# Transposing normalised rows with 32 by 32 squares on VectorE and DMAs through DRAM, instead of on TensorE

## The chip, the cores and the metric

The kernel runs on one core of a Trainium2 chip. The metric is the device time of one execution in microseconds (us), the median of several runs. A profiled execution gives the trace from which the rows below are taken.

## The reference

A "macaron" block on x of shape (B, L, D) = (4, 1024, 256): half a feed-forward network, a convolution over positions, half a feed-forward network, each behind a layer norm without weights.

```python
def ffn(x):                                     # weights are -1, 0 or 1, times a scale per output
    h = silu(tlin(x, w1_w, w1_s)) * tlin(x, w2_w, w2_s)      # 256 -> 1024, twice
    h = gelu(tlin(h, h1_w, h1_s))                            # 1024 -> 1024
    h = gelu(tlin(h, h2_w, h2_s))                            # 1024 -> 1024
    return tlin(h, w3_w, w3_s)                               # 1024 -> 256

def mixer(x):                                   # S4D: K is made from log_dt, A, C
    y = irfft(rfft(x^T, 2L) * rfft(K, 2L))[:, :, :L]         # along the positions
    return gelu(y^T) @ W.T + b

x = x + 0.5 * ffn(layernorm(x))
x = x + mixer(layernorm(x))
x = x + 0.5 * ffn(layernorm(x))
```

## The kernel before

**Blocks.** The 4096 positions are cut in eight blocks of 512 tokens. The first network goes over them in turn "f" (f0 to f7, from `x` to a DRAM tile `x1`), the second in turn "g" (g0 to g7, from the DRAM tile `x2` to the output). The blocks run in one loop, f0 to g7; `ffn` does one of them. A row of x (one token, 256 features) has to be normalised along its features, with tokens on the partitions, and then multiplied with weights that want features on the partitions. So each block's normalised rows are transposed.

**Positions.** A block lies in SBUF as 128 partitions of four rows (`JT` = 4). `positions` says which tokens these are: partition p holds tokens 8p to 8p+3 (first half of a sequence, even blocks) or 8p+4 to 8p+7 (second half). The mixer `mix(b)` uses the same places: its result rows j, j+1 of every partition are stored to `x2` in four stores (j = 0, 2, 4, 6), so an even block of turn g reads what the first two of them wrote.

**Parts.** An fp32 activation is split in two parts that TensorE multiplies one after the other: part 0 is a cast (`fp32r`), part 1 is what the cast lost, which `low_part` computes on VectorE (L240). The tiles `xt` (two of 128x512), `ha` and `h` (eight each) have both parts. So a matmul group of a layer of 1024 inputs has 16 matmuls of 128x512.

**A block.** `ffn` issues for m = 0..7 the products pa and pb of the first layer; then layers 2 and 3, eight groups each (`p_f`, `p_g`, L267, called by `linear`); after each group ScalarE does the gelu (L299) and the cast (L301), VectorE the low part. G0 to G7 below stand for the ends of layer 3's eight groups on TensorE. Then come 64 matmuls of 128x256 for the result (`po`, L323), which take h as their stationary operand, and `finish`: scaling on VectorE, the residual's addition on POOL, a store by SP.

**What is put between.** After every group `tick()` advances one step of `aside`, the generator that makes the spectrum of the convolution's kernel (`kernel_spectrum`, beside f2 to f4) and then runs `mix(0)` to `mix(3)`; sometimes also a step of `weight_checks`, which loads weights again (`given`) and compares them. `spectrum` loads four matrices of 256 KB (`m_m2_0` is matrix 0 of mix 2; `m_k_0` and so on, of the kernel's spectrum, come in two halves of 128 KB) on SP's queue, in the order 0, 2, 1, 3, and multiplies rows with them (`pf_m`, `pf_k`, L621: 8 matmuls, one product). The mixer's rows `xm` go through the same `norm`. During layer 3, `ahead()` advances `prepare` for the next block: `load_x` (one DMA of 512 KB), `norm` in two steps, and at the call after the last group `transposed`:

```python
pts = [bank(f"pt_{name}_{k}") for k in range(DC)]       # two PSUM banks
for k, i in order:                                       # 2 x 4 squares of 128 x 128
    nc.tensor.transpose(
        pts[k][:, i * P : (i + 1) * P], xn[:, i, k * P : (k + 1) * P], ident   # L248
    )
...
nc.vector.tensor_copy(xt[k][:, 0, :], pts[k])            # L258
last = low_part(xt[k], pts[k])                           # L240
```

The first block has no predecessor; its transposes come ahead of the loop. The execution takes the branch with split parts; a second branch without them is for other weights.

**Order.** A scheduler fixes the order on every engine when the kernel is built, from the program's order and its own estimate of when each piece will be ready. At run time each engine, and each queue of DMAs that SP issues, goes strictly through its list. A tile pool has a limited number of buffers for a tag (`xb` three, `half` 19, PSUM eight banks).

Of the kernel before, what the change touches and what calls it, by code (L numbers as in the profile page):

```python
# [11 lines left out]
F32 = mybir.dt.float32  # L12
# [5 lines left out]
P = 128  # L18
B, L, D = 4, 1024, 256
HID = 1024  # L20
J = L // P
DC = D // P
KH = HID // P
TB = 512
JT = TB // P
N2 = 32
DD = D // 2

# [65 lines left out]
def macaron_layers(  # L94
# [23 lines left out]
    nc = tc.nc  # L118
    split = bad is not None
    wide = F32R if split else F32  # L120
    parts = 2 if split else 1
    keep = ctx.enter_context(tc.tile_pool(name="keep", bufs=1))
    work = ctx.enter_context(tc.tile_pool(name="work", bufs=2))
    small = ctx.enter_context(tc.tile_pool(name="small", bufs=2))
    dram = ctx.enter_context(tc.tile_pool(name="dram", bufs=1, space=bass.MemoryType.DRAM))
# [6 lines left out]
    def half(name, *shape, dtype=F32):  # L132

        return work.tile([P, *(shape or (512,))], dtype, tag="half", name=name, bufs=19)

    def ring(name, *shape, dtype=F32):

        return work.tile([P, *shape], dtype, tag="ring", name=name, bufs=15)
# [5 lines left out]
    ident = keep.tile([P, P], F32, name="ident")  # L144
# [12 lines left out]
    x1 = dram.tile([B, L, D], F32, name="x1")  # L157
    x2 = dram.tile([B, L, D], F32, name="x2")

    k_hat = dram.tile([2 + len(PAIRS), 2, P, 2, D], F32, name="k_hat")  # L160

    def column(i):
# [2 lines left out]
    def positions(t, b, j, n=2):  # L165
        return t[b].rearrange("(p j) d -> p j d", j=J)[:, j : j + n, :]

    def load_x(t, blk, name, queue=nc.sync):
        b, g = divmod(blk, J // JT)
        xb = work.tile([P, JT, D], F32, tag="xb", name=name, bufs=3)  # L170
        queue.dma_start(xb, positions(t, b, g * JT, JT))
        return xb

    def rows(w):
# [4 lines left out]

    x_first = work.tile([P, JT, D], F32, tag="xb", name="x_f0", bufs=3)  # L180
    for i, queue in ((0, nc.sync), (2, nc.scalar)):
        queue.dma_start(x_first[:, i : i + 2, :], positions(x, 0, i))
    eps = small.tile([P, 1], F32, name="eps", bufs=1)
    nc.vector.memset(eps, EPS)

# [52 lines left out]
    def low_part(t, src):  # L238

        return tt(t[:, 1, :], src, t[:, 0, :].bitcast(F32), ALU.subtract)  # L240

    def transposed(xn, name, first=False):


        pts = [bank(f"pt_{name}_{k}") for k in range(DC)]
        order = [(k, i) for k in range(DC) for i in range(JT)]
        for k, i in sorted(order, key=lambda o: o[1]) if first else order:
            nc.tensor.transpose(  # L248
                pts[k][:, i * P : (i + 1) * P], xn[:, i, k * P : (k + 1) * P], ident
            )  # L250
        xt = [ring(f"xt_{name}_{k}", parts, TB, dtype=wide) for k in range(DC)]
        last = None
        if first:
            last = nc.vector.tensor_copy(xt[0][:, 0, :], pts[0])  # L254
            nc.scalar.copy(xt[1][:, 0, :], pts[1])
        for k in range(DC):
            if not first:
                nc.vector.tensor_copy(xt[k][:, 0, :], pts[k])  # L258
            if split:
                last = low_part(xt[k], pts[k])  # L260
        return (xt, last) if first else xt

    def linear(ps, w, m, acts):
        n = len(acts)
# [10 lines left out]
    def ffn(xt, src, dst, blk, name, tick, ahead, final):  # L275

        ha = []
        for m in range(KH):  # L280
            pa, pb = bank(f"pa_{name}_{m}"), bank(f"pb_{name}_{m}")
            linear(pa, w1_sb, m, xt)
            linear(pb, w2_sb, m, xt)
            g = half(f"g_{name}_{m}")
            t = ring(f"ha_{name}_{m}", parts, TB, dtype=wide)
            nc.scalar.activation(g, pa, AF.Silu, scale=sc_sb[:, 0, m : m + 1])  # L286
            stt(g if split else t[:, 0, :], pb, sc_sb[:, 1, m : m + 1], g, ALU.mult, ALU.mult)
            if split:
                nc.scalar.copy(t[:, 0, :], g)
                low_part(t, g)  # L290
            ha.append(t)
        for layer, w in ((2, h1_sb), (3, h2_sb)):
            hb = []
            for m in range(KH):
                ps = bank(f"p{layer}_{name}_{m}")
                linear(ps, w, m, ha)
                t = ring(f"h{layer}_{name}_{m}", parts, TB, dtype=wide)
                g = half(f"g{layer}_{name}_{m}") if split else t[:, 0, :]
                nc.scalar.activation(g, ps, AF.Gelu, scale=sc_sb[:, layer, m : m + 1])  # L299
                if split:  # L300
                    nc.scalar.copy(t[:, 0, :], g)  # L301
                    low_part(t, g)
                hb.append(t)
                if layer == 3:
                    ahead()
                if m < KH - 1:
                    tick()
            ha = hb
        ahead(last=True)
        tick()  # L310
        b, g = divmod(blk, J // JT)
        rest = []
        for i in range(0, JT, 2):
            xr = half(f"xr_{name}_{i}", 2, D)
            nc.sync.dma_start(xr, positions(src, b, g * JT + i))
            rest.append(xr)

        def result(ps, i, n):

            for e in range(n):  # L320
                for k in range(KH):
                    for part in range(parts):
                        nc.tensor.matmul(  # L323
                            ps[:, e * D : (e + 1) * D],
                            ha[k][:, part, (i + e) * P : (i + e + 1) * P],
                            w3_sb[:, k, :],
                            start=(k == 0 and part == 0),
                            stop=(k == KH - 1 and part == parts - 1),
                        )

        def finish(ps, y, xr, i, n, add_on):
            stt(
                y,
                ps.rearrange("p (e d) -> p e d", e=n),
                0.5,
                w3s_sb[:, None, :].to_broadcast([P, n, D]),
                ALU.mult,
                ALU.mult,
            )
            add_on.tensor_tensor(y, xr, y, ALU.add)  # L340
            nc.sync.dma_start(positions(dst, b, g * JT + i, n), y)

        for i in range(0, JT, 2):
            y = half(f"y_{name}_{i}", 2, D)
            if final and i + 2 == JT:
                for e in range(2):
                    ps = bank(f"po_{name}_{i + e}")
                    result(ps, i + e, 1)
                    finish(
                        ps[:, 0:D],  # L350
                        y[:, e : e + 1, :],
                        rest[i // 2][:, e : e + 1, :],
                        i + e,
                        1,
                        nc.vector,
                    )
            else:
                ps = bank(f"po_{name}_{i}")
                result(ps, i, 2)
                finish(ps, y, rest[i // 2], i, 2, nc.gpsimd)  # L360
# [336 lines left out]

    def mix(b):

        xn = [load_x(x1, 2 * b + g, f"xm_{b}_{g}") for g in range(2)]  # L700
        yield
        for g in range(2):
            yield from norm(xn[g], f"m{b}_{g}")
# [18 lines left out]
        r, i = factors(0)  # L722
# [6 lines left out]
        for n, (p, q) in enumerate(PAIRS):  # L729
            r, i = following  # L730
# [25 lines left out]
        c, e = (add(by[1, 7], by[5, 3], op, t) for op, t in ((ALU.add, "c"), (ALU.subtract, "e")))  # L756
        d, f = (add(by[3, 5], by[7, 1], op, t) for op, t in ((ALU.add, "d"), (ALU.subtract, "f")))
# [3 lines left out]
        g, h = half(f"g_i{b}", 2, D), half(f"h_i{b}", 2, D)  # L761
# [13 lines left out]
        for j in range(JQ):  # L775
            r = swapped(w[j]) if j == 2 else w[j]
            for sign in (1.0, -1.0):
                o = half(f"v{j}_{sign < 0}_{b}", 2, D)
# [24 lines left out]
        for j in range(0, J, 2):  # L803
            xr = half(f"xr_{b}_{j}", 2, D)
# [13 lines left out]
            y = half(f"yw_{b}_{j}", 2, D)  # L818
# [13 lines left out]
    done = []  # L832

    def prepare(turn, blk, upcoming):

        name = f"{turn}{blk}"
        if turn == "f":

            queue = weights_from if blk < 4 else nc.sync
            xb = x_second if blk == 1 else load_x(x, blk, f"x_{name}", queue)  # L840
        else:
            while ("m", blk // 2) not in done:
                next(aside, None)
            xb = load_x(x2, blk, f"x_{name}")
        yield
        yield
        for _ in norm(xb, name):
            yield
            yield
        while True:  # L850
            if ("last layer", blk, turn) in done:
                upcoming.extend(transposed(xb, name))
                return
            yield

    def all_aside():

# [24 lines left out]
        nc.tensor.matmul(warm[:, 0:P], ident, ident, start=(i == 0), stop=(i == N_WARM - 1))  # L882
    for _ in norm(x_first, "f0", parts_of=2):
        pass
    xt, last_split = transposed(x_first, "f0", first=True)
    for n, (turn, blk) in enumerate(blocks):
        following = []
        steps = [prepare(*b, following) for b in blocks[n + 1 : n + 2]]
# [7 lines left out]
        src, dst = (x, x1) if turn == "f" else (x2, out)  # L896
# [3 lines left out]
        xt = following  # L900
# [78 lines left out]
```

## Time and profile before

| | us |
|---|---|
| median of 3 runs (1430.51 to 1431.01) | 1430.93 |
| the profiled execution | 1430.35 |
| its span, first to last instruction | 1428.6 |
| TensorE busy in it | 1416.6 |
| VectorE busy | 835.0 |
| ScalarE busy | 678.6 |
| share of the DMA engines that SP's queue used | 15.1% |

The core's granted TensorE clock was 0.999 of full speed. A busy time is the sum over an engine's records; matmuls overlap their neighbours a little, so the distance from one start to the next, in the timeline, is the better measure of what one costs. In a row of a group, `out<-in` names the tiles without their numbers, `x64` counts the instructions, then come their busy time and the mean in ns, then the idle time before them and what ended it. In the waits, the three numbers are the total in us, the number of waits and the longest. In the rows of DMA issues come the count, the size and the median time from issue to landing.

### The profile page before, as it was taken

The page shows a single profiled execution, that of the slowest core. Times are in us where ns is not written, and L with a number is a line of the kernel's source. Part 1 is how long each engine was busy: PE and PEld are TensorE (multiplying, and loading weights), DVE is VectorE, ACT ScalarE, POOL GpSimd, SP SyncE. Part 2 cuts the span into 40 slices and gives each one's busy share as a digit, 9 for nine tenths or more (in the row PEclk, how much of TensorE's full clock was granted, in tenths as well). Part 3 has the DMA queues.
Part 4 walks back from the last instruction along what each step waited for, and adds up shares of the span by engine and source line. Part 5 has one row for each costly group of instructions (what it writes and reads, how often), then busy time and mean ns, then how long its engine had stood idle before and what let it go on. Part 6 is the DMA issues. An engine that isn't in the chain of part 4 may idle for free.

```text
span 1428.6 us, 18125 instructions
## 1 busy us (share of the span) xinstructions
PE 1416.6 (99%) x7092; PEld 1199.8 (84%) x7092; DVE 835.0 (58%) x1584; ACT 678.6 (48%) x1033; POOL 81.6 (6%) x82
## 2 busy tenths in 40 slices
PE   9999999999999999999999999999999999999997
PEld 7888888888888888888888888888888888888886
DVE  6786566753836577562877633867447766341412
ACT  5875468744435435344453433534345344443432
POOL 4010000100000000020000010000010000100000
PEclk9999999999999999999999999999999999999999
DMA  9010000101122140140231130231131301200000
GB/s 372 36 45 0 31 15 1 45 4 44 69 85 67 38 134 21 60 133 16 74 96 51 45 127 15 75 96 38 60 103 59 92 35 41 92 30 1 23 8 18
DMA packets 43278, 85.50 MB, mean 60 GB/s; under 512 B 4832, under 2 KB 10208, under 8 KB 43184
## 3 DMA queue, kind: packets, MB, share of 16 engines
q1 hardware_dynamic: 38016, 70.04, 15.1%
q0 software_dynamic: 5024, 13.96, 2.8%
q8 instruction: 57, 0.93, 0.3%
q14 instruction: 37, 0.30, 0.1%
q10 hardware_dynamic: 144, 0.26, 0.1%
HBM read 69.04 MB, written 15.20 MB: 59 GB/s over the span
## 4 chain that ended last, share of the span: by engine, by line
PE 97%; DVE 1%; ACT 1%; DMA 0%; issue 0%; POOL 0%; POOLq 0%
PE p_g L267 33%; PE p_f L267 31%; PE po_g L323 4%; PE pa_f L267 4%; PE pa_g L267 4%; PE pb_f L267 4%; PE pb_g L267 4%; PE po_f L323 4%; PE pi L791 2%; PE pw L811 2%; PE pf_m L621 2%; PE pk L552 1%; PE pf_k L621 0%; PE pt_f L248 0%; PE pt_g L248 0%; PE warm L882 0%
## 5 line engine op out<-in xcount | busy, mean ns | idle before, releaser
L267 PE MATMUL p_f<-h_f,h_sb 128*128 128x512 f32 x1024 | 239.1, 392 | 0.0
L267 PE MATMUL p_f<-ha_f,h_sb 128*128 128x512 f32 x1024 | 237.7, 391 | 0.0
L267 PE MATMUL p_g<-h_g,h_sb 128*128 128x512 f32 x1024 | 236.0, 390 | 0.0
L267 PE MATMUL p_g<-ha_g,h_sb 128*128 128x512 f32 x1024 | 235.0, 390 | 0.0
L267 PEld LDWEIGHTS p_f<-ha_f,h_sb 128*128 128x128 f32 x1024 | 191.5, 188 | 40.8 <-DVE ha_f L240 0.8
L267 PEld LDWEIGHTS p_g<-h_g,h_sb 128*128 128x128 f32 x1024 | 192.3, 188 | 39.8
L267 PEld LDWEIGHTS p_g<-ha_g,h_sb 128*128 128x128 f32 x1024 | 192.1, 188 | 39.7
L267 PEld LDWEIGHTS p_f<-h_f,h_sb 128*128 128x128 f32 x1024 | 191.4, 188 | 40.0 <-DVE h_f L240 0.3
L299 ACT ACTIVATE g_g<-p_g,sc_sb 128x512 f32<-128x512 f32 x128 | 88.2, 690 | 273.5 <-PE p_g L267 267.7
L240 DVE TENSOR_TENSOR h_g<-g_g,h_g 128x512 fp32r<-128x512 f32 x128 | 88.3, 692 | 221.7 <-ACT h_g L301 221.7
L240 DVE TENSOR_TENSOR h_f<-g_f,h_f 128x512 fp32r<-128x512 f32 x128 | 88.4, 691 | 190.1 <-ACT h_f L301 189.9
L299 ACT ACTIVATE g_f<-p_f,sc_sb 128x512 f32<-128x512 f32 x128 | 88.1, 689 | 220.2 <-PE p_f L267 211.4
L301 ACT CAST h_g<-g_g 128x512 fp32r<-128x512 f32 x128 | 79.3, 620 | 3.9
L301 ACT CAST h_f<-g_f 128x512 fp32r<-128x512 f32 x128 | 79.0, 618 | 3.2
L267 PE MATMUL pa_f<-xt_f,w_sb 128*128 128x512 f32 x256 | 69.7, 391 | 0.7 <-DVE xt_f L254 0.7
L267 PE MATMUL pb_f<-xt_f,w_sb 128*128 128x512 f32 x256 | 69.1, 389 | 0.0
L267 PE MATMUL pa_g<-xt_g,w_sb 128*128 128x512 f32 x256 | 68.6, 390 | 0.0
L267 PE MATMUL pb_g<-xt_g,w_sb 128*128 128x512 f32 x256 | 68.4, 389 | 0.0
L286 ACT ACTIVATE g_g<-pa_g,sc_sb 128x512 f32<-128x512 f32 x64 | 43.4, 689 | 52.6 <-PE pa_g L267 49.7
L323 PE MATMUL po_f<-w_sb,h_f 128*128 128x256 f32 x512 | 64.4, 285 | 1.3 <-ACT h_f L301 1.0
L323 PEld LDWEIGHTS po_f<-w_sb,h_f 128*128 128x128 f32 x512 | 62.4, 192 | 2.0 <-ACT h_f L301 1.2
L323 PE MATMUL po_g<-w_sb,h_g 128*128 128x256 f32 x512 | 63.7, 285 | 0.0
(230 smaller groups left out, 1636.0 us busy)
## 6 DMA issues: line engine op xcount, KB each, us to landing
h_sb<-in_h_dram POOLq DMA_DIRECT2D x8, 1024.0 KB, 13.9
given<-in_h_dram SPq DMA_DIRECT2D x32, 256.0 KB, 3.1
kr<-k_hat SPq DMA_DIRECT2D x20, 256.0 KB, 2.6
ki<-k_hat SPq DMA_DIRECT2D x20, 256.0 KB, 2.9
xr_f<-in_x_dram SPq DMA_DIRECT2D x16, 256.0 KB, 4.2
x<-y_f SPq DMA_DIRECT2D x16, 256.0 KB, 2.4
xm<-x SPq DMA_DIRECT2D x8, 512.0 KB, 4.7
m_m<-in_cosm_dram SPq DMA_DIRECT2D x16, 256.0 KB, 4.2
```

The lines of the kernel that those rows point to most:

```text
L240: return tt(t[:, 1, :], src, t[:, 0, :].bitcast(F32), ALU.subtract)
L267: nc.tensor.matmul(ps, w[:, k, m * P : (m + 1) * P], acts[k][:, part, :], start=(k == 0 and part == 0), stop=(k == n - 1 and part == parts ...
L286: nc.scalar.activation(g, pa, AF.Silu, scale=sc_sb[:, 0, m : m + 1])
L299: nc.scalar.activation(g, ps, AF.Gelu, scale=sc_sb[:, layer, m : m + 1])
L301: nc.scalar.copy(t[:, 0, :], g)
L323: nc.tensor.matmul(ps[:, e * D : (e + 1) * D], ha[k][:, part, (i + e) * P : (i + e + 1) * P], w3_sb[:, k, :], start=(k == 0 and part == 0) ...
L552: nc.tensor.matmul(pk[0:NA, at + i, :, :].rearrange("p h b -> p (h b)"), a[:, i].rearrange("p a b -> p (a b)"), qd[d1 // per_tile][:, at + ...
L621: nc.tensor.matmul(ps[e][:, part, :], m[:, e, part, :], rows_of(q + JQ * e), start=True, stop=True)
L791: nc.tensor.matmul(banks[dc][e][:, q * P : (q + 1) * P], vs[q + JQ * e][:, part, dc * P : (dc + 1) * P], m[:, e, part, :], start=(part == ...
L811: nc.tensor.matmul(ps[:, e * D : (e + 1) * D], yts[dc][j // JQ][:, (j % JQ + e) * P : (j % JQ + e + 1) * P], wt_sb[:, dc, :], start=(dc == 0),
```

## The change

The rows are no longer transposed on TensorE, but for the first block. `squares` transposes within 32 by 32 squares on VectorE (two instructions of 128x512), sends the squares to their places in a DRAM tile `moved` in eight DMAs of 64 KB (32 partitions, runs of 512 bytes), and fetches the two transposed tiles `xf` (256 KB each) from there. `parted` casts them and takes their low parts, from SBUF instead of PSUM. `squares` runs in layer 3 as soon as the rows are normalised, `parted` at the call where `transposed` was.

For this a block's tokens are arranged anew. `tokens` takes 512 adjacent tokens, four to a partition for the residual and the stores; `load_x` loads them in four DMAs of 128 KB, each filling 32 partitions. Stores of turn f, loads of turn g and the residuals follow. The mixer keeps its places (`load_half`). All DMAs of `squares` are issued by SP.

```diff
+SQ = 32
...
+    moved = dram.tile([DC, P, JT, P], F32, name="moved")
...
+    def load_half(t, b, g):
+        xb = work.tile([P, JT, D], F32, tag="xb", name=f"xm_{b}_{g}", bufs=3)
+        nc.sync.dma_start(xb, positions(t, b, g * JT, JT))
+        return xb
+
+    def tokens(t, blk, a=0, n=JT):
+        b, g = divmod(blk, J // JT)
+        rows_of = t[b, g * TB : (g + 1) * TB, :]
+        return rows_of.rearrange("(q a) d -> q a d", a=JT)[:, a : a + n, :]
+
     def load_x(t, blk, name, queue=nc.sync):
         b, g = divmod(blk, J // JT)
         xb = work.tile([P, JT, D], F32, tag="xb", name=name, bufs=3)
-        queue.dma_start(xb, positions(t, b, g * JT, JT))
+        src = t[b, g * TB : (g + 1) * TB, :].rearrange("(j s a) d -> a s j d", s=SQ, a=JT)
+        for a in range(JT):
+            queue.dma_start(xb[a * SQ : (a + 1) * SQ], src[a])
         return xb
...
-        queue.dma_start(x_first[:, i : i + 2, :], positions(x, 0, i))
+        queue.dma_start(x_first[:, i : i + 2, :], tokens(x, 0, i, 2))
...
-    def transposed(xn, name, first=False):
+    def transposed(xn, name):
...
+    def squares(xn, name):
+        out = []
+        for k in range(DC):
+            sq = half(f"sq_{name}_{k}", P // SQ, JT, SQ)
+            nc.vector.transpose(
+                sq, xn[:, :, k * P : (k + 1) * P].rearrange("p j (c r) -> p c j r", r=SQ)
             )
+            for a in range(JT):
+                nc.sync.dma_start(
+                    moved[k].rearrange("(c r) a q -> a r c q", r=SQ)[a],
+                    sq[a * SQ : (a + 1) * SQ].rearrange("r c j s -> r c (j s)"),
+                )
         for k in range(DC):
+            t = half(f"xf_{name}_{k}")
+            nc.sync.dma_start(t, moved[k].rearrange("d a q -> d (a q)"))
+            out.append(t)
+        return out
+
+    def parted(xf, name):
+        xt = []
+        for k, src in enumerate(xf):
+            t = ring(f"xt_{name}_{k}", parts, TB, dtype=wide)
+            nc.vector.tensor_copy(t[:, 0, :], src)
             if split:
-                last = low_part(xt[k], pts[k])
-        return (xt, last) if first else xt
+                low_part(t, src)
+            xt.append(t)
+        return xt
...
-            nc.sync.dma_start(xr, positions(src, b, g * JT + i))
+            nc.sync.dma_start(xr, tokens(src, blk, i, 2))
...
-            nc.sync.dma_start(positions(dst, b, g * JT + i, n), y)
+            nc.sync.dma_start(tokens(dst, blk, i, n), y)
...
-        xn = [load_x(x1, 2 * b + g, f"xm_{b}_{g}") for g in range(2)]
+        xn = [load_half(x1, b, g) for g in range(2)]
...
         for _ in norm(xb, name):
             yield
-            yield
-        while True:
-            if ("last layer", blk, turn) in done:
-                upcoming.extend(transposed(xb, name))
-                return
-            yield
+        xf = squares(xb, name)
+        while ("last layer", blk, turn) not in done:
+            yield
+        upcoming.extend(parted(xf, name))
```

More of the change, by code (lines that the diff above doesn't have):

```diff
@@ L240, in low_part @@
         return tt(t[:, 1, :], src, t[:, 0, :].bitcast(F32), ALU.subtract)
-    def transposed(xn, name, first=False):
+    def transposed(xn, name):
         pts = [bank(f"pt_{name}_{k}") for k in range(DC)]
[L246 to L249, printed above, removed]
-            )
[L251 to L255, printed above, removed]
-        for k in range(DC):
-            if not first:
-                nc.vector.tensor_copy(xt[k][:, 0, :], pts[k])
+        for i in range(JT):
+            for k in range(DC):
+                nc.tensor.transpose(
+                    pts[k][:, i * P : (i + 1) * P], xn[:, i, k * P : (k + 1) * P], ident
+                )
+        xt = [ring(f"xt_{name}_{k}", parts, TB, dtype=wide) for k in range(DC)]
+        last = nc.vector.tensor_copy(xt[0][:, 0, :], pts[0])
+        nc.scalar.copy(xt[1][:, 0, :], pts[1])
+        if split:
+            for k in range(DC):
+                last = low_part(xt[k], pts[k])
+        return xt, last
@@ new lines, in squares @@
+    def squares(xn, name):
+        out = []
+        for k in range(DC):
+            sq = half(f"sq_{name}_{k}", P // SQ, JT, SQ)
+            nc.vector.transpose(
+                sq, xn[:, :, k * P : (k + 1) * P].rearrange("p j (c r) -> p c j r", r=SQ)
+            )
+            for a in range(JT):
+                nc.sync.dma_start(
+                    moved[k].rearrange("(c r) a q -> a r c q", r=SQ)[a],
+                    sq[a * SQ : (a + 1) * SQ].rearrange("r c j s -> r c (j s)"),
+                )
+        for k in range(DC):
+            t = half(f"xf_{name}_{k}")
+            nc.sync.dma_start(t, moved[k].rearrange("d a q -> d (a q)"))
+            out.append(t)
+        return out
@@ L310, in ffn @@
         tick()
-        b, g = divmod(blk, J // JT)
         rest = []
@@ L884, in macaron_layers @@
         pass
-    xt, last_split = transposed(x_first, "f0", first=True)
+    xt, last_split = transposed(x_first, "f0")
     for n, (turn, blk) in enumerate(blocks):
```

## The prediction

> **What bounds the kernel now.** I read the page's first part, then the chain that ended last. Together they say that time is TensorE's.
>
> ```profile
> PE 1416.6 (99%) x7092; PEld 1199.8 (84%) x7092; DVE 835.0 (58%) x1584; ACT 678.6 (48%) x1033; POOL 81.6 (6%) x82
> PE 97%; DVE 1%; ACT 1%; DMA 0%; issue 0%; POOL 0%; POOLq 0%
> ```
>
> Next the waits of TensorE: these four are all there are, 4.6 us together.
>
> ```profile
> PE warm L882 <- POOL ident masks.py:199: 2.6, 1, 2.6
> PE po_f L323 <- ACT h_f L301: 1.0, 1, 1.0
> PE pa_f L267 <- DVE xt_f L254: 0.7, 1, 0.7
> PE po_f L323 <- DVE h_f L240: 0.3, 1, 0.3
> ```
>
> So work taken off TensorE shortens the run by its own length, and any wait put before TensorE lengthens it by its own. Then the groups by shape, for the transposes, and the timeline at a block's end (start, duration, engine, line).
>
> ```profile
> L248 PE MATMUL pt_f<-ident,x_f 128*128 128x128 f32 x64 | 8.9, 287 | 0.0
> L248 PE MATMUL pt_g<-ident,x_g 128*128 128x128 f32 x64 | 8.3, 272 | 0.0
> ```
>
> ```profile
> 1319.70 12.41 PE L267 MATMUL p_g<-h_g,h_sb 128*128 128x512 f32 x54
> 1331.95 1.04 PE L248 MATMUL pt_g<-ident,x_g 128*128 128x128 f32 x8
> 1332.74 7.92 PE L323 MATMUL po_g<-w_sb,h_g 128*128 128x256 f32 x64
> ```
>
> The groups sum to 17.2 us for 128 transposes, but records overlap: the result product starts 0.79 us after the first of eight transposes. Start to start is the true price.
>
> [...]128 KB stores land in 1.8 us, 256 KB stores in 2.4.[...]
>
> **A. Removed from TensorE.** Blocks f0 to g6 prepare a successor: 15 boundaries of 8 transposes. Their start-to-next-start, one by one in the timeline, is 0.79 to 0.97 us; the sum is 12.6. Only the first block's 8 transposes stay. VectorE's PSUM casts and low parts become SBUF ones, same number and size: nothing.
>
> **B. The new path, and what is queued behind it.** Per boundary: two VectorE transposes of 128x512, eight SP writes, two SP fetches. Every 128x512 VectorE pass takes 0.60 us start to start, so 0.6 each (below that nothing speaks; twice as much, 1.2, is my upper bound). Back-to-back stores on SP stand 0.5 us apart (386.97, 387.50, 388.44, 388.99, 389.49, 389.94; 0.32 at least). With t0 the first square's start: the first write goes at t0+0.75, the eighth at t0+4.25, the first fetch at t0+4.75; the eighth lands 1.8 later, so the second fetch, which waits for it on SP, goes at t0+6.1, and the next DMA of the queue at **t0+6.6**. The fetched rows land at t0+8.7. After the change VectorE's order has the squares behind the low part of layer 3's fourth group (end G3; low parts end 2.2 us after the group, so t0 = G3+2.2) and the casts that read the rows behind that of its seventh (G3+13.1): 2.2 us to spare. The fetch itself is hidden, except where rows come late. What is not hidden is the queue: SP issues in order, and the mixer's matrices stand right behind the second fetch in three kinds of block.
>
> ```profile
> m_m<-in_cosm_dram SPq DMA_DIRECT2D x16, 256.0 KB, 4.2
> ...
> k_hat<-x_k SPq DMA_DIRECT2D x15, 128.0 KB, 1.8
> ...
> m_k<-in_cosm_dram SPq DMA_DIRECT2D x8, 128.0 KB, 2.8
> ```
>
> - f3, beside f4's preparation: m_k_2, in two halves, is issued at t0+6.6 and 7.1 and lands 2.8 later: G3+12.1. TensorE wants it after two groups (3.63 each) and one matrix product (1.54): G3+8.9. Stall 3.2 (2.4 to 5).
> - g1: m_m2_2 the same way with 3.5 to land (2.8 to 4.2): G3+12.3 against G3+8.9. Stall 3.4 (2.4 to 6).
> - g3: this is the worst. The timeline of g3 (q is a queue's issue):
>
> ```profile
> 1045.43 0.32 SPq L826 DMA_DIRECT2D x<-yw  x1
> 1045.86 0.37 SPq L171 DMA_DIRECT2D x_g<-x  x1
> 1046.74 0.32 SPq L826 DMA_DIRECT2D x<-yw  x1
> ...
> 1047.59 0.48 SPq L610 DMA_DIRECT2D m_m<-in_cosm_dram  x1
> ...
> 1060.01 1.89 PE L621 MATMUL pf_m<-xm,m_m 128*128 128x256 f32 x8
> ```
>
> Today the next rows' load goes out one store before the last, and the matrix 12.4 us before its use. With adjacent tokens the load needs all four stores: last issued 1046.74, landed 1049.4; four pieces of it landed about 1054.0. On VectorE statistics, one weight check and the mixer's statistics (4.1), the low part (0.6) and the scaling (1.6) follow: t0 = 1060.3. The first matrix is behind the second fetch: issued 1066.9, landed 1070.4, wanted 1060.0. Stall **10.4** (7.5 to 13).
>
> **C. The boundary f7 to g0.** Here VectorE is late even now:
>
> ```profile
> 707.89 2.40 PE L323 MATMUL po_f<-w_sb,h_f 128*128 128x256 f32 x18
> 710.63 5.78 PE L323 MATMUL po_f<-w_sb,h_f 128*128 128x256 f32 x46 [0.34 <-DVE h_f L240]
> ```
>
> 18 result matmuls cover the last low part, which arrives 0.34 us too late. After the change, 11.6 us of VectorE work stand between two low parts of layer 3 (g1's and the mixer's statistics and scalings among them), against 7.6; by the rows' durations the last low part is ready 8.4 us after the groups' end instead of 3.5. In TensorE's order after the change, 28 result matmuls (0.125 each) and three of the next block (0.227 each) stand ahead of its reader and cover 4.2. New stall, less the 0.34 there is: about 4.0 (2.5 to 5).
>
> **D. Smaller.** At f0 0.5, at f5 0.9 (statistics and products behind late mixer rows), at g0 0.3: 1.7 (0 to 4). **At nothing:** x loads in four pieces of 128 KB (three on POOL's queue at the start, 1.65 us more issue, hidden since the first weights of layer 2 land some 3 us before use); blocks of adjacent tokens for residual and stores (same bytes; DMA's share is 15%); 150 more SP issues of 0.5 us, other than those ordered before a matrix.
>
> **Sum** against the profiled execution's own 1430.35 (span 1428.6): -12.6 + 3.2 + 3.4 + 10.4 + 4.0 + 1.7 = +10.1, so 1440.5. That execution lies 0.6 below the median shown, 1430.93: **1441.0**.
>
> **Rivals.**
> - R1, the other side: the queue is quicker than its rows. With issues at 0.32 and landings at 1.2, matrices come 2.1 to 3 us sooner; with x_g4's pieces landing as one 512 KB load does today (3.7 us, 1 us sooner) and C half as large, B is 0.9 + 0.6 + 5.9 and C 2.0, with D at 0: 9.4 us against 12.6, so 1427.7; with C wholly covered 1425.7; with the matrices never late 1418 to 1420. I take 1424 as its middle. It decides from the point where new waits total less than 12.6. For it: SP issues at 0.32 alone. Against: its stores in a row at 0.5, and m_m landings of 2.8 to 6.7.
> - R2, slower still: writes of 512-byte runs cost more than full rows. No store before has such runs. With stages 2 us later, B's three stalls grow by 6, and the rows of g6, whose load waits for a last store issued at 1230.54 and which come with 0.4 to spare by the same sum, become late by 1.6: 1448.6.
> - R3: the waits just eat the gain (they total 9.8 to 15.4): 1428 to 1434, no change.
>
> That the change doesn't do what it says is excluded: only 8 transposes remain in TensorE's order.
>
> **How the numbers follow.** The measurement tells some 0.2%, 2.9 us. My own case, with the bounds of B to D, 1434 to 1447: chance 0.57. R2 0.13, R1 0.20, R3 0.10 (of which 0.08 within 0.2%). Slower: 0.57 + 0.13 + 0.02 = 0.72; same 0.08; faster 0.20. The range runs from R1's 1424 to R2's 1449; outside lie R1's far end and R2's tail, under 0.2.
>
> **What would show it.** Right: TensorE gets waits at the matrix products (pf_m, pf_k) released by DMAs of m_m and m_k, about 3 us in f3 and g1 and 10 in g3; a wait of result matmuls on VectorE at f7; SP's own queue waiting at the writes for VectorE and at the fetches; no pa waiting on xt; PE busy near 1404. Wrong: SP's next issue well under 6 us after the squares, x_g4 landed before 1052, squares over 1.2 us, or pa waits at many boundaries, which would mean that the fetch is not hidden at all.

## The result, and the profile after

The changed kernel takes **1462.8 us** (median; 1461.11 to 1463.28) against 1430.82: ratio 1.0222, 95% interval 1.0204 to 1.0239. The sign was forecast; the size, +10 us with a range up to 1449, was not: it is +32. The profiled execution took 1462.53 us (span 1460.8), 32.2 more than that of before.

The page's busy times and its chain that ended last, after:

```profile
PE 1418.2 (97%) x6972; PEld 1197.8 (82%) x6972; DVE 839.0 (57%) x1614; ACT 682.4 (47%) x1037; POOL 87.6 (6%) x91
PE 89%; DVE 3%; DMA 3%; ACT 2%; SPq 1%; issue 1%; POOL 0%; DVEq 0%; POOLq 0%
```

TensorE runs 120 matmul records fewer and yet is busy 1.6 us longer. The records removed summed to some 16 us, so others became longer by about as much. That is the first odd thing to follow up. The chain now passes through DMAs and SP's queue. The waits of TensorE (total, number, longest), where four rows stood before:

```profile
PE pf_m L664 <- DMA m_m<-in_cosm_dram: 13.2, 2, 9.0
PE p_bad L435 <- DVE total L433: 4.8, 1, 4.8
PE pf_k L664 <- DMA m_k<-in_cosm_dram: 4.7, 1, 4.7
PE po_f L366 <- DVE h_f L257: 3.0, 4, 1.1
PE pa_g L311 <- DVE xt_g L301: 2.6, 1, 2.6
PE warm L923 <- POOL ident masks.py:199: 2.6, 1, 2.6
PE pa_f L311 <- DVE xt_f L301: 1.3, 1, 1.3
PE po_f L366 <- ACT h_f L345: 1.3, 1, 1.3
...
```

With two more rows of 0.7 and 0.2 they make 34.4 us, 29.8 more than before. The place with the longest one is g3. Its timeline, SP's queue, one row of VectorE and TensorE:

```profile
1063.38 2.07 SPq L188 DMA_DIRECT2D x_g<-x  x4
...
1074.56 3.70 SPq L286 DMA_DIRECT2D moved<-sq_g  x8
1075.65 1.38 DVE L244 TENSOR_SCALAR xm<-xm,mv_m,rstd_m 128x256 f32<-128x256 f32 x4
1078.49 0.34 SPq L292 DMA_DIRECT2D xf_g<-moved  x1
1078.88 0.42 SPq L188 DMA_DIRECT2D x_g<-x  x1
1079.63 0.34 SPq L292 DMA_DIRECT2D xf_g<-moved  x1
1080.07 0.38 SPq L653 DMA_DIRECT2D m_m<-in_cosm_dram  x1
...
1085.06 3.75 PE L664 MATMUL pf_m<-xm,m_m 128*128 128x256 f32 x8 [9.01 <-DMA m_m<-in_cosm_dram]
```

The matrix is issued last, behind the eight writes and both fetches, and TensorE stands 9.01 us for it. (VectorE's row is the last other thing that this product needs: it has scaled the mixer's rows by 1077.03, 1.0 us after TensorE stopped.) But look at the product itself: its eight records take 3.75 us, where the same row took 1.89 before. The stretches of two us there (length, busy time, granted clock, DMA share, GB/s) say why:

```profile
1078.00:1080.00 2.00, 0.00 (x0) 1.00 0.55 103
1080.00:1082.00 2.00, 0.00 (x0) 0.52 0.90 222
...
1086.00:1088.00 2.00, 2.00 (x6) 0.50 1.08 228
1088.00:1090.00 2.00, 2.00 (x6) 0.50 1.03 361
1090.00:1092.00 2.00, 2.00 (x10) 0.92 0.25 96
```

TensorE stands from 1076.05; 4.0 us later the granted clock falls to 0.50, and TensorE works on at half speed for 5 us more, to 1090.33. I summed, over stretches of 1 us, busy time times the missing share of the clock. That gives 1.7 us at f0, 1.6 at f3, 1.7 at f7, 3.1 at g1, 2.6 at g3 and 2.8 behind p_bad in g4: **13.5 us**, where the kernel before has none. So: -12.6 for the transposes, +29.8 of waits, +13.5 of half clock are +30.7, of 32.2 measured.

### The profile page after: what moved, and what is told of

The parts are those of the page before. It is cut to its first block, busy times and chain, and to the rows that moved or that the text cites. A ratio compares the mean times of both kernels' runs of the same rounds, so it can differ in the third digit from the quotient of the medians.

```text
span 1460.8 us, 18295 instructions
## 1 busy us (share of the span) xinstructions
PE 1418.2 (97%) x6972; PEld 1197.8 (82%) x6972; DVE 839.0 (57%) x1614; ACT 682.4 (47%) x1037; POOL 87.6 (6%) x91
## 4 chain that ended last, share of the span: by engine, by line
PE 89%; DVE 3%; DMA 3%; ACT 2%; SPq 1%; issue 1%; POOL 0%; DVEq 0%; POOLq 0%
PE p_g L311 30%; PE p_f L311 27%; PE po_g L366 4%; PE pa_f L311 4%; PE pa_g L311 4%; PE pb_f L311 4%; PE pb_g L311 4%; PE po_f L366 3%; PE pf_m L664 2%; PE pi L834 2%; PE pw L854 2%; PE pk L595 1%; SPq L286 1%; DMA m_m<-in_cosm_dram 1%; PE pf_k L664 0%
## 5 line engine op out<-in xcount | busy, mean ns | idle before, releaser
L366 PEld LDWEIGHTS po_f<-w_sb,h_f 128*128 128x128 f32 x512 | 65.7, 198 | 6.4 <-DVE h_f L257 3.9
```

Source lines behind the costliest of these rows:

```text
L366: nc.tensor.matmul(ps[:, e * D : (e + 1) * D], ha[k][:, part, (i + e) * P : (i + e + 1) * P], w3_sb[:, k, :], start=(k == 0 and part == 0) ...
```

## The experiments

My theory by then: the path over DRAM is short enough, but its ten DMAs per boundary stand in SP's queue ahead of loads that others need soon, and each stall that this makes is paid twice, as a wait and as half clock. The rivals: the layout of adjacent tokens; a path that is too long anywhere; a clock that falls for reasons of its own; a cost at every boundary.

### The transposes left out, nothing in their place

```diff
+        if not first:
+            flat = xn.rearrange("p j d -> p (j d)")
...
+                src = flat[:, k * TB : (k + 1) * TB]
+                nc.vector.tensor_copy(t[:, 0, :], src)
+                if split:
+                    low_part(t, src)
...
+            return xt
```

> The kernel before with its 120 later transposes left out and nothing in their place: the first layer's parts are cast straight from the normalised rows, which lie the wrong way, so the network's values are meaningless; everything else is issued as before. It prices step A alone. My theory (the 12.6 us of start-to-start distances are TensorE's to lose): 1430.9 - 12.6 = 1418. Rival (TensorE spends that time anyway, waiting at the block's end for the last low part, which the transposes covered): 0.5 to 0.8 us per boundary are lost again, 1424 to 1430.

1419.21 us against 1430.64 on the same chip: ratio 0.9925 (0.9909 to 0.9942), so **-11.4 us**. No half clock, and the waits are 5.8 us against 4.6. Step A stands: what the distances gave as 12.6 is 11.4 net of new waits. This is also about the most that an arrangement of the squares can gain.

### The layout alone

`turned` does the eight transposes on TensorE and then calls `parted` on the two PSUM banks.

```diff
-        src = t[b, g * TB : (g + 1) * TB, :].rearrange("(j s a) d -> a s j d", s=SQ, a=JT)
-        for a in range(JT):
-            queue.dma_start(xb[a * SQ : (a + 1) * SQ], src[a])
+        queue.dma_start(xb, tokens(t, blk))
...
-        xf = squares(xb, name)
+            yield
         while ("last layer", blk, turn) not in done:
             yield
-        upcoming.extend(parted(xf, name))
+        upcoming.extend(turned(xb, name))
```

> The changed kernel's blocks of adjacent tokens alone: rows loaded in one DMA of 512 KB, four tokens to a partition, and transposed on TensorE as before. No squares, no DMAs through DRAM. My theory (the loss comes from the new DMAs ahead of others in SP's queue): the layout costs only the later load of even blocks in turn g, 0 to 3 us: 1431 to 1434. Rival (the layout is what costs: in g3 the load stands behind the last store of the mixer, and VectorE waits for it): half of the 32 us or more, above 1445.

1429.89 against 1430.64: ratio 0.9997 (0.9989 to 1.0006). Adjacent tokens alone cost nothing that this interval shows, the load behind the mixer's last store included. That rival falls. (A block is loaded in one DMA here; what the four pieces of the changed kernel cost is not priced apart.)

### The matrices on POOL's queue

```diff
-                nc.sync.dma_start(
+                nc.gpsimd.dma_start(
                     m[o * (P // over) : (o + 1) * (P // over)],
```

> The changed kernel with one edit: the matrices m_m and m_k are loaded by POOL's queue, so they no longer stand behind the squares' writes and fetches on SP's. My theory (a place in SP's queue is all that makes them late, and TensorE's clock falls to half after each such wait): the three waits of 4.7, 4.2 and 9.0 us at the matrix products go, and some 7 us of half clock behind them: 1462.8 - 25 = 1438 (1436 to 1444). Rival (the transfers are late because the DMA engines are busy with 64 KB writes of 512-byte runs): the waits stay, 1458 or more.

1445.25 (1443.18 to 1446.56): -17.5, where I expected -25. No row of TensorE's waits names a matrix any more. At g1 and g3 POOL's queue issues the matrices before the squares' writes begin (at g3 from 1048.26, the first write at 1065.02), so this prices their place in SP's queue; it does not show that the DMA engines could deliver them beside the writes. In the changed kernel that question hardly arises at g3: the last write had landed by 1079.57, before the matrix was issued. What is left at g3 is a different wait. TensorE's waits, and then the timeline there, POOL's and SP's queues and VectorE:

```profile
PE pf_m L664 <- issue: 3.6, 1, 3.6
```

```profile
1048.26 1.61 POOL L653 DMA_DIRECT2D m_m<-in_cosm_dram  x3
1049.23 2.29 SPq L188 DMA_DIRECT2D x_g<-x  x4
...
1058.30 0.75 DVE L234 BATCH_NORM_STATS2 stats_g<-x_g 128x6 f32<-128x256 f32 x2 [5.30 <-DMA x_g<-x]
...
1065.68 1.38 DVE L244 TENSOR_SCALAR xm<-xm,mv_m,rstd_m 128x256 f32<-128x256 f32 x4
```

VectorE stands 5.30 us for g4's rows, and the mixer's rows that the same product needs come behind them. (TensorE's row names no releaser; that it is these rows I infer from the times: the scaling ends at 1067.) The rows are late because of this edit, as it seems: beside the matrices that POOL's queue sends just before (the DMA share is 0.82 to 1.17 from 1049 to 1057), their four pieces, issued by 1051.52, hold VectorE until 1058.30, 6.8 us later. In the changed kernel the pieces landed in 2.6 us by the median, and VectorE went on 2.3 us after the last issue (1065.45 and 1067.76). There the mixer's rows were ready 8 us before the matrix. So the 9.0 us at g3 came from the matrix and its place in SP's queue, and this edit put 3.6 new ones in their stead.

### Idle work in the waits

```diff
+FILL = {("k", 2): 10, ("m2", 2): 10, ("m3", 0): 22}
...
+                    for _ in range(FILL.get((name, q), 0)):
+                        nc.tensor.matmul(ps[0][:, 0, :], ident, bias_sb, start=True, stop=True)
```

> The changed kernel with idle work for TensorE put in its three longest waits: 10, 10 and 22 matmuls of 128x256 (0.385 us each by the row of the matrix products, so 3.9, 3.9 and 8.5 us) into the bank that the late product overwrites, right ahead of it. No wait gets shorter. Theory that the clock falls because TensorE stands idle: the half-clock stretches behind these three waits (some 2, 2.8 and 2.6 us lost) go, 1462.8 - 7 = 1456. Rival (the clock falls for another reason, the load on the chip or the DMAs in flight): the stretches stay, 1462 to 1466.

1457.44 (1456.6 to 1457.9): **-5.4 us by giving TensorE more to do**. The half-clock stretches at f3, g1 and g3 are gone from the profile; those at f0, f7 and behind p_bad stay (5.0 us together). At f3 the filling was too short by one wait, without half clock behind it:

```profile
PE pf_k L668 <- DMA m_k<-in_cosm_dram: 1.9, 1, 1.9
```

In this run the half clock goes where TensorE has work in the wait, with the same DMAs in number and size: at f3, g1 and g3 the changed kernel lost 1.6, 3.1 and 2.6 us to it, this run nothing.

### Stalls of known length, in the kernel before

```diff
+                    for _ in range(n_held - 1):
+                        nc.gpsimd.tensor_tensor(late, late, late, ALU.subtract)
+                    held = nc.tensor.matmul(held_ps[:, 0:P], ident, late[:, 0:P], start=True, stop=True)
...
+                with tc.issue_after(held.ins) if held is not None else nullcontext():
                     linear(ps, w, m, ha)
```

> The kernel before with six stalls of TensorE put in, in layers 2 and 3 of g5, g6 and g7: after the fourth group a small matmul reads a tile that a chain of 0, 1, 2, 3, 5 and 8 POOL operations makes from the group's gelu, and the next group stands behind it. Nothing else changes. By POOL's row of 1.27 us an operation the stalls are 1.0, 2.3, 3.6, 4.9, 7.4 and 11.2 us, 30.4 together. Theory that a stall of about 3 us and more also halves the clock for 3 to 6 us of work: half-clock stretches behind the last three or four, 1.6 to 2.8 us lost in each, 1468 to 1472. Rival (idle time costs itself and no more): no stretch, 1461.

(The 3 us of this theory are an estimate from the two profiles above: half clock stood behind single waits of 2.6 to 9.0 us in the changed kernel, and none behind the wait of 1.9 us left in the run with idle work.)

1473.38 us, a single execution: +43 against the profiled execution before, just above the range that I gave. Five of the six stalls in TensorE's timeline (the sixth, with no POOL operation, was 0.8 us):

```profile
1241.44 0.49 PE L313 MATMUL held_g<-late_g,ident 128*128 128x128 f32 x2 [2.75 <-POOL late_g L309]
...
1298.98 0.49 PE L313 MATMUL held_g<-late_g,ident 128*128 128x128 f32 x2 [3.34 <-POOL late_g L311]
...
1334.58 0.80 PE L313 MATMUL held_g<-late_g,ident 128*128 128x128 f32 x2 [4.46 <-POOL late_g L311]
...
1396.83 0.79 PE L313 MATMUL held_g<-late_g,ident 128*128 128x128 f32 x2 [6.70 <-POOL late_g L311]
...
1438.93 0.80 PE L313 MATMUL held_g<-late_g,ident 128*128 128x128 f32 x2 [10.05 <-POOL late_g L311]
```

Behind 0.8 us there was no half clock; behind the five the loss was 1.7, 1.7, 3.1, 2.7 and 2.2 us. Even 2.75 us can be enough. Its stretches:

```profile
1240.00:1241.00 1.00, 0.00 (x0) 1.00 0.00 0
1241.00:1242.00 1.00, 0.56 (x3) 0.92 0.00 0
1242.00:1243.00 1.00, 1.00 (x4) 0.50 0.06 16
...
1245.00:1246.00 1.00, 1.00 (x5) 0.88 0.00 0
```

The clock is still full at the end of the stall (1241.44) and falls 0.4 us after work has resumed, at a DMA share of 0.00 to 0.06. Waits of 28.1, 11.4 of half clock, some 2 of the added matmuls and 1.2 of small waits elsewhere make 42.7 of the 43 us. Each of these five stalls costs its length and 1.7 to 3.1 us more, with no steady rise from 2.75 to 10.05 us of stall.

### The sum of the weight checks later

```diff
+        for _ in range(4):
+            yield
         total = small.tile([P, 1], F32, name="total")
```

> The changed kernel with only the sum of the weight checks (total, p_bad) traced four steps of the checks later. My theory: the 4.8 us wait of p_bad and 2.8 us of half clock behind it go: 1462.8 - 7.6 = 1455. Rival (VectorE's backlog in g4 makes the next matmuls wait as long, whoever stands first): the wait turns up at the result product po behind it, 1460 to 1463.

1455.55 (1453.82 to 1456.33): -7.3, as expected: the p_bad wait and its half clock are gone. The moved steps shift SP's list a little; the two matrix waits became 16.1 us together (13.2 before) at less half clock (1.4 us at g1 and 1.9 at g3, 3.1 and 2.6 before).

### SP relieved of three things

With the matrices on POOL's queue and the sum later, as in the two edits above:

```diff
-            queue = weights_from if blk < 4 else nc.sync
+            queue = weights_from
```

> The changed kernel with three edits: matrices loaded by POOL's queue, the rows of f4 to f7 too, and the sum of the weight checks traced later. The squares stay on SP. My theory: against the kernel with the matrices on POOL (1445.3) the late rows in f0 (3.6 us of waits, 1.7 of half clock) and the p_bad wait (4.8 and 2.7) go: 1445.3 - 12.8 = 1432.5 (1430 to 1437). Rival (each wait removed lets another one behind it show): less than half of that, above 1439.

1440.02 (1436.07 to 1442.96), -5.2 against the matrices alone; I expected -12.8. In the profile, which is the fastest of these runs, the p_bad wait is gone; f0 still waits 3.1 us, now for ScalarE, and g3 3.0 us as in the run with the matrices alone. Here the rival was right: one cause removed, another showed.

### The squares on ScalarE's queue

```diff
-                nc.sync.dma_start(
+                nc.scalar.dma_start(
                     moved[k].rearrange("(c r) a q -> a r c q", r=SQ)[a],
...
-            nc.sync.dma_start(t, moved[k].rearrange("d a q -> d (a q)"))
+            nc.scalar.dma_start(t, moved[k].rearrange("d a q -> d (a q)"))
```

> The changed kernel with the squares' eight writes and two fetches per boundary issued by ScalarE's queue instead of SP's. My theory (the places in SP's queue behind the squares are what costs): the waits at the matrix products and the late rows of f0 go, with their half clock, 25 to 30 us; but ScalarE now waits for VectorE's squares and for their landing, some 6 us per boundary in the middle of layer 3, and its gelu evictions come late; where three groups are enough to catch up, nothing is left: 1430 to 1440. Rival (the path through DRAM is too long wherever it is issued): rows come late at the first layer (pa waits on xt at many boundaries), above 1455.

1472.11 (1469.23 to 1473.02), slower still, against both expectations: no rows late at many boundaries, yet the matrices late again (16.2 us of waits, 17.9 in the changed kernel). What makes it slower still stands elsewhere: the result products wait 6.9 us for ScalarE, which now issues the squares' DMAs (1.3 in the changed kernel), and p_bad 6.7 (4.8). The timeline at g3, ScalarE's queue and SP's:

```profile
1082.60 4.61 ACTq L286 DMA_DIRECT2D moved<-sq_g  x8
1083.18 1.79 SPq L188 DMA_DIRECT2D x_g<-x  x4
1087.49 0.35 SPq L653 DMA_DIRECT2D m_m<-in_cosm_dram  x1
```

The matrix now stands behind the load of g5's rows, which goes out as the squares end at 1083.16 and, it seems, needs the buffer that they free. What holds the matrix from 1085.0 to 1087.4 is not certain: the profile names a landing of those rows, and ScalarE, which could release a tile, was held by the eight writes until 1087.2. The times suggest that a queue is not a place apart: what waits in one can hold buffers that the other's loads want.

### Which boundaries pay

Squares at some boundaries, TensorE at the others, by a list of names. First the six at which the changed kernel stood go back to TensorE:

```diff
+ON_TENSOR = ("x_f1", "x_f4", "x_g0", "x_g2", "x_g4", "x_g5")
...
+        if name in ON_TENSOR:
+            queue.dma_start(xb, tokens(t, blk))
+            return xb
...
+        if f"x_{name}" in ON_TENSOR:
+            while ("last layer", blk, turn) not in done:
+                yield
+            upcoming.extend(turned(xb, name))
+            return
         xf = squares(xb, name)
```

> The changed kernel with the rows of f1, f4, g0, g2, g4 and g5 transposed on TensorE as before (loaded four adjacent tokens to a partition), and the other nine blocks' by squares and DMAs. The six are the boundaries behind which the changed kernel stood still. My theory (the loss sits wholly at the six, and a boundary whose queue and VectorE have room keeps its 0.8 us): before less 9 x 0.8, 1430.8 - 7 = 1423.5 (1422 to 1426). Rival (every boundary pays; where the six were relieved, waits move to others): 1430 or more.

1429.12, ratio 0.9995 (0.9986 to 1.0003): the loss is gone, but no gain is left that stands clear of the noise. Expected was 1423.5. At f2 the same thing had come up once more, VectorE's and TensorE's timelines:

```profile
256.38 0.43 DVE L238 BATCH_NORM_STATS2 stats_m<-xm 128x6 f32<-128x256 f32 x1 [4.52 <-DMA xm<-x]
```

```profile
260.78 0.74 PE L379 MATMUL po_f<-w_sb,h_f 128*128 128x256 f32 x4 [1.26 <-DVE h_f L261]
```

The load of the mixer's rows stands between f3's two fetches; VectorE waits 4.52 us for it, with low parts behind; 1.7 us of waits and 1.7 of half clock follow. These 3.4 are more than half of the 5.6 us that are missing; the rest is open.

The opposite list:

```diff
+ON_TENSOR = ("x_f2", "x_f3", "x_f5", "x_f6", "x_f7", "x_g1", "x_g3", "x_g6", "x_g7")
```

> The opposite share: squares and DMAs only for f1, f4, g0, g2, g4 and g5, TensorE for the nine others. My theory: all that the change lost and only six fifteenths of its gain: 1462.8 + 9 x 0.8 = 1470 (1464 to 1474). Rival (the loss is spread, each of 15 boundaries paying some 2 us): 1430.8 + 6 x 2.1 = 1443.5.

1473.02 (1472.36 to 1474.68), ratio 1.0300 (1.0284 to 1.0316): the six boundaries carry all of the loss.

With the matrices on POOL's queue, a shorter list:

```diff
+ON_TENSOR = ("x_f1", "x_g0", "x_g4", "x_g5")
```

> The matrices loaded by POOL's queue as in the run with that edit alone, and TensorE's transposes only for f1, g0, g4 and g5: f4 and g2 keep their squares. My theory (at these two the place in SP's queue was the whole cause): nothing waits for a matrix, 11 boundaries keep 0.8 us: 1430.8 - 8.8 = 1422 (1421 to 1425). Rival (f4's and g2's rows or POOL's own work bring other waits): over 1426.

1430.31, ratio 0.9996 (0.9988 to 1.0005), not 1422. No matrix is waited for, as expected, but f2's waits are there, and g3 has 1.9 us and 1.7 of half clock. No squares stand at g3 in this run; that g4's rows come late there, again beside the matrices that POOL's queue sends, is my estimate. The three 512 KB loads of x_g in this run landed in 4.5 us by the median, the eight of the kernel before in 3.7.

And a longer one, with SP's queue as it was:

```diff
+ON_TENSOR = ("x_f1", "x_f4", "x_g0", "x_g2", "x_g4", "x_g5", "x_f3", "x_f6")
```

> The run with nine boundaries on squares, with f3 and f6 given back to TensorE too: squares and DMAs for f2, f5, f7, g1, g3, g6 and g7, behind whose fetches SP's queue holds nothing that TensorE or VectorE needs soon. My theory (in the nine, the mixer's rows stood behind f3's fetches and VectorE waited 4.5 us for them ahead of a low part; with that gone no wait and no half clock are left over those of before): 1430.6 - 7 x 0.8 = 1425 (1424 to 1427). Rival (a boundary of squares pays about what it gains, wherever it lies): 1428.5 or more.

1428.32 (1425.91 to 1430.21) against 1430.1: ratio **0.9986** (0.9979 to 0.9993). Of the versions that still transpose every block this is the one that beats both kernels, by 1.8 us where seven boundaries should bring 5.6; 1425 was expected. The fastest run has a mean clock of 0.999, most others 0.996 to 0.998; the profiled one, the slowest, has half-clock stretches at the start and at f0 (1.7 us each). To that version one edit more:

```diff
-            queue = weights_from if blk < 4 else nc.sync
+            queue = weights_from if blk < 5 else nc.sync
```

> The run with seven boundaries on squares, and the load of f4's rows issued by POOL's queue instead of SP's, so that their statistics, which VectorE has ahead of f0's last low part, come without a wait. My theory (that load is what is left: 1.8 us of wait at pa and 1.7 us of half clock in f0): 1428.3 - 3 = 1425 (1423.5 to 1426.5). Rival (the seven boundaries themselves pay): 1428 or more.

1430.61, ratio 1.0000 (0.9992 to 1.0008): missed. f4's load was not the rest; pa at f0 still waits 1.6 us for xt. Set beside that of the run above, its profile shows something else. Both have two waits at f0, 0.95 and 1.80 us in the first, 0.95 and 1.63 in the second, but half clock follows in the first alone. It depends on how the idle time falls into the slots of 3.41 us that the last section works out: 2.67 us lie in one slot in the first profile, and 1.30 and 1.28 in two slots in the second. That this can change from one execution to the next may be why the times scatter more than those of before. In the first profile the wait of 1.8 us and the half clock of 3.4 take 5.2 of the 5.6 us, and its span is 0.3 us below that of the kernel before; in the second the wait alone takes 1.6, and the span is 2.5 below. There is no steady cost after the last matmul: from VectorE's last operation to the end of the span it is 5.7 us in the first, 7.7 in the second and 6.5 in the kernel before.

### One boundary given back at a time

```diff
+ON_TENSOR = ("x_g4",)
```

> The changed kernel with g4's rows alone transposed on TensorE: in g3 no squares stand in SP's queue ahead of the mixer's matrices; the block of adjacent tokens and the load behind four stores stay. My theory (the queue and VectorE's order behind the squares make g3's stall): its wait of 9.0 us and 2.6 us of half clock go, 0.9 us of transposes come back: 1462.8 - 10.7 = 1452 (1450 to 1454). Rival (the later load of adjacent tokens makes the stall): half or more of it stays, over 1457.

1449.62 (1448.19 to 1450.47): -13.2 from one boundary. The stall at g3 and its half clock are gone though the load still stands behind all four stores. The rows held nothing up: TensorE is busy and its clock full in every us from 1055 to 1086. So the squares' DMAs ahead of the matrices made g3's stall, and not the later load.

```diff
+ON_TENSOR = ("x_g0",)
```

> The changed kernel with g0's rows alone transposed on TensorE. Squares read x_g0 in the middle of layer 3 and free its buffer there, so g1's rows are loaded 10 us sooner and VectorE normalises them ahead of f7's last low parts. My theory: with g0 on TensorE the buffer comes free at the block's end, those 5 us of VectorE work move behind the low parts, and the waits in f7 (0.5 and 2.6 us) and 1.65 us of half clock go, against 0.8 us of transposes: 1462.8 - 4 = 1459 (1457.5 to 1460). Rival (the mixer's statistics are VectorE's backlog, whatever frees the buffer): the waits stay, 1462 or more.

1459.29 (1457.41 to 1462.84): -3.5, as expected; f7's half clock is gone and with it the 2.6 us wait of pa. So the squares of g0 bring step C's backlog, but not through the buffer that I named: g1's load goes out 18.8 us before the end of layer 3 in both runs, and in the changed kernel (at 695.25) before the squares read x_g0 (at 703.29). What differs is VectorE's order. In the changed kernel g1's scaling and the mixer's, at 708.39 and 709.89, stand ahead of f7's last low parts; with g0 on TensorE they come behind them. Why the order comes out so is open.

## Why the prediction was wrong in size

- **A, -12.6:** -11.4 with nothing in the transposes' place.
- **B, the chain:** right, nearly to the digit. In g3 the squares start at 1073.82; the first write came at +0.74 (0.75 forecast), the first fetch at +4.67 (4.75), the next DMA of the queue at +6.25 (6.6). Squares cost here what other passes of the same shape cost, as I had estimated from VectorE's rows before: 687 to 689 ns a record in the groups by shape, where the low parts of h have 690. The 64 KB writes of 512-byte runs landed in 1.7 us by the median, the 128 KB stores of before in 1.7 and 1.8 (k_hat), so R2's ground did not show though the time lay beyond R2. R1's landings of 1.2 us were an assumption: the shortest of k_hat's stores before took 1.7.

```profile
L282 DVE STREAM_TRANSPOSE sq_g<-x_g 128x512 f32<-128x512 f32 x16 | 10.4, 687 | 0.1
```

- **B, the stalls:** f3 3.2 forecast, 4.7 measured; g1 3.4 and 4.2; g3 10.4 and 9.0. The sum 17.0 became 17.9. At g3 the cause was the one I named, but the size is in part luck: the rows came sooner than forecast, so the squares began 2.2 us before TensorE wanted the product and not 0.3 after, while the matrix took 4.9 us to land and not 3.5.
- **C, 4.0:** 0.5 at po and 2.6 at pa, less the 0.34 of before: 2.8. The longer list on VectorE was right; it goes when g0's squares go.
- **D, 1.7:** short. f0 alone has 3.6 us of waits against 1.0 before. VectorE has f4's statistics ahead of a low part, and f4's load stands between and behind the fetches:

```profile
83.75 0.75 DVE L234 BATCH_NORM_STATS2 stats_f<-x_f 128x6 f32<-128x256 f32 x2 [3.16 <-DMA x_f<-in_x_dram]
```

- **Not in the sum, p_bad:** 4.8 us. I looked at low parts, rows and matrices as what TensorE waits for in layer 3, and not at the weight checks' one matmul, ahead of which VectorE's order in g4 had grown.
- **Not in the sum, the clock:** this is the step that failed. "Work taken off TensorE shortens the run by its own length, and any wait put before TensorE lengthens it by its own" is wrong in its second half. Six stalls cost 13.5 us more than their length. The trace of before, on which the sentence rests, has no such price: its longest wait behind the first matmuls is 1.0 us, and its clock stays full up to the last. In the runs the granted clock falls to 0.50, each time for 1.4 to 3.2 us of loss, that is 3 to 6 us of work at half speed, and a stall of 2.75 us was enough for it (the last section says more).

The new waits were 7.1 us more than the 22.7 forecast and the clock 13.5: together 20.6 of the 22.1 us by which the sum was short.

## What to carry to other kernels

In these traces a stall that left TensorE idle for 2.0 us or more of one 3.41-us slot (49 of 49) had a price on top of its length, mostly 1.7 us and at most 3.2, with no steady growth with the stall (1.7 us behind a stall of 2.75, 2.2 behind one of 10.05). By these figures several such stalls are worse than one long one of the same sum; idle matmuls in three waits brought 5.4 us back. When work moves to DMAs, walk the issuing queue and every in-order engine behind it, and ask of each load that now stands later who takes it next and what stands behind that. And a queue that relieves another sends its own transfers at other times: with the matrices on POOL's queue, VectorE stood 5.30 us for g4's rows, and 0.49 in the changed kernel.

## What the hardware showed that I had not expected

The half clock set in behind stalls of 2.75 us, and at f0 behind three waits of 0.98, 1.27 and 1.32 us with 0.5 us of work between each; behind a single wait of 0.8 us it did not. In the run where matmuls fill the waits of g1 and g3 (4.2 and 9.0 us before), the clock stays at 1.00 there.

The traces also show why the length alone doesn't decide. In the 13 of them with more than one fall of the clock (of 16, all but that of the layout alone) the falls lie multiples of 3.41 us apart, to within 0.02 us, and each half-clock stretch ahead of the last matmuls lasts one to four times 3.41. In the changed kernel it falls at 90.22, 349.64, 721.69, 892.36, 1080.09 and 1185.90 us; the distances are 76, 109, 50, 55 and 31 times 3.413. I divided the 16 traces into such slots and counted TensorE's idle time in each, from 12 us on and up to the last matmuls. Every full-clock slot with 2.0 us or more idle was followed by one at half clock (49 of 49). No slot with up to 1.5 us idle was, and of the seven between, at 1.53 to 1.89, three were. So a stall of 2.75 us can fall into one slot or be split over two, and in these traces the price comes in whole slots: half of what TensorE works in them, 1.7 us for a full one.

Eight DMAs of 64 KB in runs of 512 bytes took SP 3.7 us to issue and landed in 1.7 us each by the median, no later than stores of 128 KB before (k_hat, 1.7 and 1.8).
